# Two-layer decoder: the second batch's expert rows are gathered inside the first self unit, and VectorE alone normalizes the first batch

## The chip, the core and the metric

The kernel runs on one core of a Trainium2 chip. A core has a tensor engine for matrix products (PE, TensorE), a vector engine (DVE, VectorE), a scalar engine for activation functions (ACT, ScalarE), a general engine (POOL, GpSimd) and a sync engine (SP, SyncE) whose work here is to issue transfers. Each engine runs its own list of instructions in order and meets the others only through semaphores. Transfers (DMA) run beside them on 16 DMA engines. Products land in PSUM, eight banks of 128 x 512 floats here, and are copied ("evicted") to SBUF by ACT or DVE.

The metric is device time in microseconds (us). Before the change it is 2070.02 us, the median of three runs from 2069.47 to 2071.17. A difference of about 0.2% (4.1 us) is what a measurement of this kernel can tell from none.

## The reference, cut to what matters

All data are float32, with 4 batches of 512 tokens of width 256 and a second sequence ("context") of 1601 rows.

```python
x = layernorm(x + L0_attn(x))                       # a learning rule run over the tokens
x = layernorm(x + L0_xattn(x, ctx))                 # attention over the context
x = layernorm(x + L0_ffn(x))                        # 8 experts, the best 2 of each token
x = layernorm(x + L1_attn(x, w_qkv, w_out))         # causal self attention, 16 heads of 16
x = layernorm(x + L1_xattn(x, ctx, mask, ...))      # attention over the context, rotated, 16 heads
x = layernorm(x + L1_ffn(x))
```

The change sits at the seam between the third line and the fourth. The expert layer ends with a weighted sum of two rows per token,

```python
probs = softmax(xf @ Wr + br);  topw, topi = top_k(probs, 2);  topw = topw / sum(topw)
out[t] = topw[t, 0] * y[topi[t, 0], t] + topw[t, 1] * y[topi[t, 1], t]
```

and x + out is normalized (mean and variance over the 256 columns) before it becomes the input of the self attention,

```python
q, k, v = x @ w_qkv.T
attn = softmax(q @ k.T * 0.25 + causal_bias)        # per batch and head, 512 x 512
```

## The kernel before, in words

**Up to the seam.** The expert layer computes only the rows that were chosen and leaves them in memory (`ys`). The last layer is the function `last_layer` (line 1264). Its instructions are put out in an order written out by hand: what the Python code calls first stands first in each engine's list.

**Units.** The last layer is 32 units, each a batch and a group of 4 heads: first 16 self units (4 batches x 4 groups), then 16 cross units. This text counts them from 0, so units 0 to 3 are the first batch's self attention and unit 4 is the second batch's first. A self unit has 4 steps, one for each 128 keys. A step computes transposed scores of two heads at a time (`scores`, line 1572), adds the causal mask on the diagonal, takes the exponential on ACT (line 1582) and then the weighted sum of values on PE (`weighted`, line 1601).

The exponential needs the row maximum of the scores, so each unit's scores are also computed once ahead only for the maximum: 8 maximum steps per self unit (`slot1`, PE tile `most`, line 207; DVE lines 1531 and 1533), followed by `negated` (line 1546), which takes the maxima together and writes them by SP into the spare row of the query tile. The maximum steps run 4 steps ahead of the unit's end. So the first four maximum steps of unit n are issued in the second half of unit n-2 and the other four in the first half of unit n-1.

**Work between the steps.** Three lists belong to each unit. `starts` is done at its beginning (mostly loads by SP). `extras` is PE work spread evenly over its steps. `quiet` is work for other engines, one entry after each half step and the rest at the end. All of it stands in the same lists of the engines as the unit's own steps; nothing is moved later by a scheduler.

**What a batch needs before its self units.** `combined(b)` (line 1312) gathers the two expert rows of each token with indirect DMAs issued by POOL (line 1318), adds them with their weights on DVE (lines 1332 and 1345), normalizes (`normalize_apart`, line 152) and turns the result so that the width lies on the partitions: eight transposes on PE in two halves (line 1353), each half copied to SBUF by ACT (line 1356). In `normalize_apart` DVE counts the statistics, ACT takes the root by a logarithm and an exponential (`rstd_ln`, line 127) and ACT applies scale and shift (line 176). `rstd_newton` (line 135) is a root of twelve small DVE instructions used elsewhere in the kernel.

Then `self_rows(b, c)` (line 1371) computes keys and queries of half c of the heads (groups 2c and 2c+1), evicts them on ACT and writes them to memory by SP (`ksd`, `qd`, line 1293). A later load by SP (line 1296), the function `rows`, brings them back arranged by head into the tiles `ks` and `qt` of a group. The loads of half c overwrite the tiles of the batch before. `self_values(b)` (line 1388) makes the four value tiles.

**The start of the layer** (lines 1875 to 1901). POOL issues 8 gathers of the first batch and then 8 of the second. Meanwhile PE and ACT make the values and some keys of the context for the first batch: `context`, with `key` items evicted by ACT (line 1437) and then rotated on DVE or POOL (lines 1403 to 1406), and `value` items evicted by ACT (line 1451). Between them stands the load of ACT's function table (line 1886). Then comes one chain of the first batch in this order: two key items, the additions with statistics and the normalization, a key item, the turn, key and query products of half 0, a key item, the load of their rows. Behind it stand the context keys' rotations and writes, the batch's values, the additions of the second batch and the first eight value items of the next context. Then unit 0 begins with its first maximum steps.

**The later batches.** The second batch is normalized in the quiet list of unit 0, turned and multiplied (half 0) in the extras of unit 1, and its rows of half 0 are loaded at the start of unit 2. Its values and half 1 are in the extras of units 2 and 3, and the rows of half 1 are loaded at the start of unit 4. The third and fourth batches gather a quarter of the tokens at a time (`asked`, `summed`, two small buffers) in the quiet lists of two earlier units, with everything after that placed alike.

Of the kernel before, what the change touches and what calls it, by code (L numbers as in the profile page):

```python
# [17 lines left out]
P = 128  # L18
# [23 lines left out]
def decoder(ctx: ExitStack, tc: tile.TileContext, a: dict, out: bass.AP):  # L42
# [65 lines left out]
    def moments(r, n=NT):  # L108
        st = small.tile([P, NT, 6], F32, tag="st", name="st")
        mv = small.tile([P, NT, 2], F32, tag="mv", name="mv")[:, :n]  # L110
        for t in range(n):
            nc.vector.bn_stats(st[:, t, :], r[:, t, :])
        for t in range(n):
            nc.vector.bn_aggr(mv[:, t, :], st[:, t, :])
        return mv

# [1147 lines left out]
    def last_layer(causal):  # L1264

        with ExitStack() as s4:
# [45 lines left out]
            def combined(b):  # L1312

                ws = picks[b]

                def gather(y, t, k):
                    i = (2 * b + k) * NT + t
                    nc.gpsimd.indirect_dma_start(
                        y, None, ys, bass.IndirectOffsetOnAxis(ap=yrows[:, i : i + 1], axis=0)
                    )  # L1320

                def fetched(h):
                    y = p4.tile([P, 2, 512], F32, tag="ex", name="ex", bufs=4)
                    y = y.rearrange("p k (t d) -> p k t d", d=D)
                    for t in range(2):
                        for k in range(2):
                            gather(y[:, k, t, :], 2 * h + t, k)
                    state["y", b, h] = y

                def added(t):  # L1330
                    for k in range(2):
                        nc.vector.scalar_tensor_tensor(
                            out=x[b][:, t, :], in0=state["y", b, t // 2][:, k, t % 2, :],
                            scalar=ws[:, k, t : t + 1], in1=x[b][:, t, :], op0=ALU.mult, op1=ALU.add,
                        )

                def asked(t):
                    y = p4.tile([P, S], F32, tag="part", name="y").rearrange("p (k d) -> p k d", d=D)
                    for k in range(2):
                        gather(y[:, k, :], t, k)  # L1340
                    state["y", b, t] = y

                def summed(t):
                    for k in range(2):
                        nc.vector.scalar_tensor_tensor(
                            out=x[b][:, t, :], in0=state["y", b, t][:, k, :],
                            scalar=ws[:, k, t : t + 1], in1=x[b][:, t, :], op0=ALU.mult, op1=ALU.add,
                        )

                def turned(c):  # L1350
                    ps = one()
                    for t in range(NT):
                        nc.tensor.transpose(  # L1353
                            ps[:, t * P : (t + 1) * P], x[b][:, t, c * P : (c + 1) * P], ident
                        )
                    nc.scalar.copy(xT[b][:, c, :], ps)

                turns = [lambda c=c: turned(c) for c in range(2)]
                stats, pairs, ends = normalize_apart(x[b])
                if b > 1:  # L1360
                    ask = [lambda t=t: asked(t) for t in range(NT)]
                    add = [lambda t=t: summed(t) for t in range(NT)]
                    none = [lambda: None]
                    order = ask[:2] + none + add[:1] + ask[2:3] + add[1:2] + ask[3:] + none + add[2:3] + none + add[3:]
                    return order, pairs + ends, turns
                fetch = [lambda h=h: fetched(h) for h in range(2)]
                if b:
                    return fetch, [lambda t=t: added(t) for t in range(NT)], pairs + ends, turns
                return fetch, [lambda t=t: (added(t), stats(t)) for t in range(NT)] + ends, turns

            def self_rows(b, c, tile=raw_tile):

# [474 lines left out]

            for b in range(1, B):
                i = index[b - 1, 0, False]
                summed, *first_sums, normal, turn = combined(b)  # L1850
                if b == 1:
                    fetch1, (add1,) = summed, first_sums
                else:
                    quiet[i - 2] += summed[:8]
                    quiet[i - 1] += summed[8:]
                quiet[i] += normal
                for c in range(2):
                    items, rows = self_rows(b, c)
                    extras[i + 1 + 2 * c] += (turn if c == 0 else []) + items
                    starts[i + 2 + 2 * c].append(rows)  # L1860
                extras[i + 2] += self_values(b)
            for b in range(B):
                i = index[b - 1, 0, True] if b else index[B - 1, 0, False]
                for c in range(2):
# [14 lines left out]
            vals.append(values_tile(p4c, "v1", NKT, nc.vector))  # L1879
            for f in fetch:  # L1880
                f()
            for f in fetch1:
                f()
            for f in context(0, (), range(4), here=qt + kself):
                f()
            nc.scalar.preload_act_table_set(EXP_AND_LN)
# [9 lines left out]
            order = [apart(f) for f in keys0[0:2]] + add + [apart(keys0[4])] + turn + [k0_, q0_, apart(keys0[5]), rows0]  # L1896
            for f in order:
                f()
            for f in turns0 + self_values(0) + add1 + values1[:8]:
                f()  # L1900
            cosT, sinT = (p4c.tile([P, S2], F32, tag=n, name=n) for n in ("c_cos", "c_sin"))

# [263 lines left out]
```

## Time and profile before

| | |
|---|---|
| median of three runs | 2070.02 us (2069.47 to 2071.17) |
| the profiled execution's own time | 2090.35 us |
| its span | 2088.6 us |
| PE busy | 2020.8 us (97%) |
| DVE busy | 1144.2 us (55%) |
| ACT busy | 1082.4 us (52%) |
| POOL busy | 550.0 us (26%) |
| mean granted clock of PE | 0.983 |

In the span the last layer's start, from the first gather on POOL to the first maximum step on PE, runs from 893.52 to 937.64 us. Units 0 to 3 begin with their scores at 953.03, 972.94, 995.38 and 1016.36, unit 4 at 1037.5, so a self unit takes about 21 us. The start and these units are all that the change touches directly: some 145 us of the 2088.6.

A timeline's row gives start and duration in us, engine and line, operation, the tile written and the tiles read, shapes, how many equal instructions in a row it holds, and in brackets the idle time before and who ended it. A releaser "remote" is one that the trace could not put down to an instruction. SPq and ACTq are the DMA issues of these two engines. The page's row PEclk is the clock that the chip granted to PE, in tenths of full speed.

### The profile page before, as it was taken

The numbers are of one execution on the slowest core, as the hardware profiler recorded it, in microseconds if no ns is written. First come the engines' busy times: TensorE is split into PE (matmuls) and PEld (weight loads), VectorE is DVE, ScalarE is ACT, GpSimd is POOL, SyncE is SP. The second block draws the span as 40 slices with busy tenths as digits, with TensorE's granted clock in tenths as the row PEclk, the third lists the DMA queues.
The fourth block names the chain that finished last, engine by engine and source line by source line (L and its number), as shares of the span: only waits on it lengthen the run. The fifth ranks groups of instructions, "written<-read, shape, count | busy, mean of one in ns | idle before, by whom it ended". The sixth has DMA issues, their size and how long they took to land.

```text
span 2088.6 us, 34219 instructions
## 1 busy us (share of the span) xinstructions
PE 2020.8 (97%) x13090; PEld 1255.9 (60%) x13090; DVE 1144.2 (55%) x2845; ACT 1082.4 (52%) x2268; POOL 550.0 (26%) x504
## 2 busy tenths in 40 slices
PE   8999999998999999979999999999999999999998
PEld 5868677777998999954555554333333333333366
DVE  2434334451333233346666677777777878888234
ACT  1211222224564555534445535788778888888731
POOL 2010001121222222123410013465455344433100
PEclk9999999999999999999999989999999999999999
DMA  9910411116887786633421210112110111102000
GB/s 374 335 50 1 160 63 52 51 61 245 304 312 283 260 321 256 265 117 109 123 62 38 72 49 26 37 43 82 64 53 28 34 54 48 32 17 72 11 11 32
DMA packets 78990, 240.52 MB, mean 115 GB/s; under 512 B 14039, under 2 KB 36989, under 8 KB 66909
## 3 DMA queue, kind: packets, MB, share of 16 engines
q1 hardware_dynamic: 58828, 139.36, 19.5%
q0 software_dynamic: 13152, 85.64, 10.7%
q10 hardware_dynamic: 6832, 13.20, 1.9%
q8 instruction: 107, 1.75, 0.3%
q14 instruction: 71, 0.57, 0.1%
HBM read 192.37 MB, written 56.69 MB: 119 GB/s over the span
## 4 chain that ended last, share of the span: by engine, by line
PE 51%; DVE 2%; ACT 2%; DMA 1%; issue 1%; another core or an unknown queue 1%; SPq 0%; ACTq 0%; POOL 0%; DVEq 0%; POOLq 0%
PE s L1572 13%; PE one L207 12%; PE po L1601 12%; PE most L207 11%; PE one L1632 1%; PE s L1588 1%; ACT x L176 1%; DVE pm L1531 0%; PE one L1657 0%; DMA kcd<-raw 0%; DVE most L1533 0%; ACT ex L1582 0%; PE one L1353 0%; DVE st L161 0%
## 5 line engine op out<-in xcount | busy, mean ns | idle before, releaser
L1582 ACT ACTIVATE ex<-s 128x512 f32<-128x512 f32 (+4 forms) x1088 | 522.5, 565 | 231.2 <-PE s L1588 123.2
L1531 DVE TENSOR_REDUCE pm<-most 128x1 f32<-128x512 f32 x768 | 478.4, 683 | 104.6 <-PE most L207 103.2
L207 PE MATMUL most<-kc,qt 32*128 32x512 f32 (+1 forms) x2048 | 434.4, 538 | 1.3 <-ACT ot L1611 0.9
L1572 PE MATMUL s<-qt,kc 32*128 32x512 f32 (+1 forms) x1664 | 410.6, 618 | 0.0
L1618 POOL TENSOR_TENSOR ot<-ot,part 128x512 f32<-128x512 f32 x180 | 228.3, 1269 | 316.6 <-ACT part L1617 316.4
L1572 PEld LDWEIGHTS s<-qt,kc 32*128 32x128 f32 (+1 forms) x1664 | 134.3, 180 | 170.8 <-ACT ex L1582 122.2
L1601 PE MATMUL po<-ex,v 128*32 128x512 f32 (+1 forms) x1664 | 225.2, 605 | 0.4 <-ACT ex L1582 0.4
L207 PEld LDWEIGHTS most<-kc,qt 32*128 32x128 f32 x2048 | 174.6, 187 | 59.1 <-issue 20.8
L1062 DVE TENSOR_TENSOR g<-g,sg 128x1024 f32<-128x1024 f32 (+1 forms) x38 | 45.5, 1197 | 217.1 <-ACT sg L1060 217.1
L1533 DVE CUSTOM_DVE_ANT_0 most<-most,c_diagq 128x384 f32<-128x384 f32 (+3 forms) x256 | 118.6, 520 | 47.6 <-PE most L207 29.4
L207 PE MATMUL wide<-xbT,eWi 128*128 128x128 f32 (+1 forms) x928 | 136.7, 308 | 3.7 <-DVE xbT L1028 3.7
L207 PE MATMUL wide<-xbT,eWg 128*128 128x128 f32 (+1 forms) x928 | 133.7, 304 | 1.5 <-ACT g L1060 1.5
L207 PEld LDWEIGHTS wide<-xbT,eWi 128*128 128x128 f32 x928 | 127.0, 194 | 12.5 <-DVE xbT L1028 3.9
L207 PE MATMUL bank<-eWo,g 128*128 128x256 f32 x592 | 130.8, 379 | 0.0
L207 PEld LDWEIGHTS wide<-xbT,eWg 128*128 128x128 f32 x928 | 124.6, 191 | 8.3 <-ACT g L1060 1.7
L1601 PEld LDWEIGHTS po<-ex,v 128*32 128x32 f32 (+1 forms) x1664 | 34.5, 108 | 150.4 <-ACT ex L1582 144.9
L207 PEld LDWEIGHTS bank<-eWo,g 128*128 128x128 f32 x592 | 111.1, 190 | 14.4
L1617 ACT COPY part<-po 128x512 f32<-128x512 f32 x180 | 106.8, 594 | 7.1 <-PE po L1601 6.1
L1572 PE MATMUL s<-qt,ks 32*128 32x128 f32 (+3 forms) x512 | 106.4, 493 | 2.5 <-DVE pm L1533 0.8
L207 PE MATMUL most<-ks,qt 32*128 32x256 f32 (+3 forms) x512 | 89.9, 486 | 3.6 <-ACT v L1451 2.3
L1060 ACT ACTIVATE g<-wide,eWi 128x128 f32<-128x128 f32 (+1 forms) x232 | 70.6, 412 | 40.1 <-PE wide L207 39.5
L207 PE MATMUL wide<-ctxT,q 128*128 128x400 f32 (+1 forms) x256 | 88.7, 499 | 1.1 <-ACT xT L201 1.1
(331 smaller groups left out, 2843.8 us busy)
## 6 DMA issues: line engine op xcount, KB each, us to landing
xs<-zero SPq DMA_DIRECT2D x32, 512.0 KB
kc<-kcd SPq DMA_DIRECT2D x16, 800.5 KB
eWo<-in_eWo SPq DMA_DIRECT2D x8, 1408.0 KB
eWi<-in_eWi SPq DMA_DIRECT2D x8, 1028.0 KB
eWg<-in_eWg SPq DMA_DIRECT2D x8, 1028.0 KB
qt<-qd SPq DMA_DIRECT2D x32, 256.0 KB
ctxT<-in_ctxT SPq DMA_DIRECT2D x4, 1601.0 KB
kcd<-in_c_rowkc SPq DMA_DIRECT2D x4, 1601.0 KB
```

Of the source, the lines that this page charges most:

```text
L176: nc.scalar.activation(into(t), xb[:, t, :], AF.Identity, scale=mid["rs"][:, t : t + 1], bias=mid["nb"][:, t : t + 1],)
L207: nc.tensor.matmul(ps, l, r, start=(i == 0), stop=(i == n - 1))
L1060: nc.scalar.activation(dst[:, k, :], pv[:, k, :], func, bias=bias)
L1062: nc.vector.tensor_tensor(part, part, dst, ALU.mult)
L1531: nc.vector.tensor_reduce(pm[:, t, j, c : c + 1], ps, AX.X, ALU.max)
L1533: nc.vector.tensor_tensor_reduce(out=ps[:, :n], in0=ps[:, :n], in1=diagq[:, 384 - t * P : 384 - t * P + n], scale=1.0, scalar=LOWEST, op0= ...
L1572: nc.tensor.matmul(ps[:kn, q0:], kt[rows, k * P : k * P + kn], q2[rows, q0:], start=True, stop=cross)
L1582: nc.scalar.activation(ex[:kn, h, q0:], ps[:kn, q0:], AF.Exp)
L1588: nc.tensor.matmul(ps[:, k * P : (k + 1) * P], later_[:, :P], later_[:, P:], start=False, stop=True)
L1601: nc.tensor.matmul(po[j * 32 : j * 32 + 32, q0:], (vals if cross else vself)[b % 2][:kn, k, c0 : c0 + 32], ex[:kn, j % 2, q0:], start=True ...
L1617: nc.scalar.copy(part, po)
L1618: nc.gpsimd.tensor_tensor(state["ot"], state["ot"], part, ALU.add)
```

## The change

- The first batch: the statistics are counted with the additions as before, and one step `normal` does all the rest on DVE: moments, the root of twelve small instructions, and four applications of mean and scale. ACT's two root instructions, DVE's shift and ACT's four applications go. The two copies of its turned halves move from ACT to DVE.
- The second batch: its 8 gathers and 8 additions leave the start. They take the form of the later batches, a quarter of the tokens at a time through two small buffers, in the quiet list of unit 0. The statistics and normalization, unchanged on DVE and ACT, move from unit 0 to unit 1. The turn and the key and query products of half 0 move from unit 1 to unit 2, the load of their rows from the start of unit 2 to the start of unit 3, and the values from unit 2 to unit 3. Half 1 stays where it was.
- One consequence in the arithmetic: the first four maximum steps of unit 4 are still issued in unit 2, now ahead of the load of its rows, so these maxima come from the first batch's rows. A row's maximum is only subtracted before the exponential and cancels in the division, so the function computed stays the same.

Lines behind the new function are 6 higher after the change (the transposes stand on line 1359, the turned copies on 1362), and from `combined` on 19 higher.

```diff
+    def moments_of(st):
+        mv = small.tile([P, NT, 2], F32, tag="mv", name="mv")
+        for t in range(NT):
             nc.vector.bn_aggr(mv[:, t, :], st[:, t, :])
         return mv
...
-                    nc.scalar.copy(xT[b][:, c, :], ps)
+                    (nc.scalar.copy if b else nc.vector.tensor_copy)(xT[b][:, c, :], ps)
...
-                stats, pairs, ends = normalize_apart(x[b])
-                if b > 1:
+                _, pairs, ends = normalize_apart(x[b])
+                if b:
                     ask = [lambda t=t: asked(t) for t in range(NT)]
                     add = [lambda t=t: summed(t) for t in range(NT)]
                     none = [lambda: None]
                     order = ask[:2] + none + add[:1] + ask[2:3] + add[1:2] + ask[3:] + none + add[2:3] + none + add[3:]
                     return order, pairs + ends, turns
                 fetch = [lambda h=h: fetched(h) for h in range(2)]
-                if b:
-                    return fetch, [lambda t=t: added(t) for t in range(NT)], pairs + ends, turns
-                return fetch, [lambda t=t: (added(t), stats(t)) for t in range(NT)] + ends, turns
+                def normal():
+                    mv = moments_of(sums)
+                    rs = rstd_newton(mv)
+                    for t in range(NT):
+                        nc.vector.tensor_scalar(
+                            x[b][:, t, :], x[b][:, t, :], mv[:, t, 0:1], rs[:, t : t + 1], ALU.subtract, ALU.mult
+                        )
+                sums = small.tile([P, NT, 6], F32, tag="st", name="st")
+                def counted(t):
+                    added(t)
+                    nc.vector.bn_stats(sums[:, t, :], x[b][:, t, :])
+                return fetch, [lambda t=t: counted(t) for t in range(NT)] + [normal], turns
...
-                summed, *first_sums, normal, turn = combined(b)
-                if b == 1:
-                    fetch1, (add1,) = summed, first_sums
+                summed, normal, turn = combined(b)
+                first = b == 1
+                if first:
+                    quiet[i] += summed
                 else:
                     quiet[i - 2] += summed[:8]
                     quiet[i - 1] += summed[8:]
-                quiet[i] += normal
+                quiet[i + first] += normal
                 for c in range(2):
                     items, rows = self_rows(b, c)
-                    extras[i + 1 + 2 * c] += (turn if c == 0 else []) + items
-                    starts[i + 2 + 2 * c].append(rows)
-                extras[i + 2] += self_values(b)
+                    n = i + 2 * c + (first and c == 0)
+                    extras[n + 1] += (turn if c == 0 else []) + items
+                    starts[n + 2].append(rows)
+                extras[i + 2 + first] += self_values(b)
...
             for f in fetch:
                 f()
-            for f in fetch1:
-                f()
...
-            for f in turns0 + self_values(0) + add1 + values1[:8]:
+            for f in turns0 + self_values(0) + values1[:8]:
                 f()
```

More of the change, by code (lines that the diff above doesn't have):

```diff
@@ L113, in moments @@
         for t in range(n):
+            nc.vector.bn_aggr(mv[:, t, :], st[:, t, :])
+        return mv
+    def moments_of(st):
+        mv = small.tile([P, NT, 2], F32, tag="mv", name="mv")
+        for t in range(NT):
             nc.vector.bn_aggr(mv[:, t, :], st[:, t, :])
```

## The prediction

> **What bounds the kernel now.** I read the page's busy lines first, then the timelines of ACT, PE and DVE where the expert layer hands over to the last layer, then SP and PE around the first units. The page says that PE is the bound, so the change is worth what PE idles less or more.
>
> ```profile
> span 2088.6 us, 34219 instructions
> ...
> PE 2020.8 (97%) x13090; PEld 1255.9 (60%) x13090; DVE 1144.2 (55%) x2845; ACT 1082.4 (52%) x2268; POOL 550.0 (26%) x504
> ```
>
> The handover holds one of the longest idle times of PE. ACT's timeline there (start, duration, engine, line, operation, names, shapes, and in brackets the idle time before and who ended it):
>
> ```profile
> 902.74 0.38 ACT L1451 COPY v<-one 128x256 f32<-128x256 f32 x1 [1.66 <-PE one L207]
> 907.68 0.37 ACT L1451 COPY v<-one 65x256 f32<-65x256 f32 x1 [4.57 <-PE one L207]
> 908.07 1.28 ACT L1886 ACT_TABLE_LOAD   x1
> 914.04 0.69 ACT L1437 ACTIVATE raw<-one,bk 128x512 f32<-128x512 f32 x1 [4.69 <-remote]
> 916.11 0.69 ACT L1437 ACTIVATE raw<-one,bk 128x512 f32<-128x512 f32 x1 [1.38 <-remote]
> 916.70 0.29 ACT L130 ACTIVATE sd<-mv,eps 128x4 f32<-128x4 f32 x1
> ...
> 917.45 2.08 ACT L176 ACTIVATE x<-x,nb,rstd 128x256 f32<-128x256 f32 x4 [0.23 <-DVE nb L171]
> ```
>
> PE and DVE in the same stretch:
>
> ```profile
> 902.24 3.60 PE L207 MATMUL one<-qt,xaK 128*128 128x512 f32 x8
> 905.67 1.88 PE L207 MATMUL one<-ks,xaK 128*128 128x512 f32 x4
> 918.10 2.16 PE L1353 MATMUL one<-ident,x 128*128 128x128 f32 x5 [10.55 <-ACT x L176]
> ...
> 906.00 0.36 DVE L166 BATCH_NORM_AGGREGATE mv<-st 128x2 f32<-128x6 f32 x4
> ```
>
> DVE has the first batch's moments at 906.36, but the root and the scaling are on ACT, behind two key evictions (L1437). By the program the second of these waits for nothing but PE's semaphore, and its matmuls stand in the rows as ended at 905.83; the signal came at 916.09. PE's signals are late in this stretch from 902 on, and the rows show such lateness again at 998, 1020, 1065 and 1089 (0.7 to 1.8 us), each time next to indirect DMAs that POOL issues (16 in a row from 893.52 to 913.35 here). Whether this lateness exists when nothing is recorded decides the case.
>
> The second place is the load of a unit's rows. SP and PE at the change from unit 1 to unit 2, where the second batch's first rows are written and read back:
>
> ```profile
> 993.87 0.62 SPq L1293 DMA_DIRECT2D ksd<-raw  x1
> 995.59 0.61 SPq L1293 DMA_DIRECT2D qd<-raw  x1
> 998.15 0.34 SPq L1296 DMA_DIRECT2D ks<-ksd  x1
> 1000.91 0.33 SPq L1296 DMA_DIRECT2D qt<-qd  x1
> ```
>
> ```profile
> 993.00 1.88 PE L207 MATMUL one<-xT,qkvQ 128*128 128x512 f32 x4
> 994.81 0.64 PE L1601 MATMUL po<-ex,vs 128*32 128x256 f32 x8
> 995.38 0.70 PE L1572 MATMUL s<-qt,ks 32*128 32x512 f32 x2
> 995.39 0.49 PE L207 MATMUL most<-ks,qt 32*128 32x128 f32 x4
> ...
> 1006.80 0.59 PE L207 MATMUL most<-ks,qt 32*128 32x384 f32 x2
> ```
>
> From the end of the query product (994.88) over its eviction, the write, and the read back to the landing of qt (1003.55 by its semaphore's count) are 8.7 us. Nothing waits for it, because the first reader of these rows is the step at 1006.80 in the third quarter of unit 2.
>
> **The change part by part.**
>
> *Start of the layer.* After: twelve small DVE operations of the Newton root, one every 0.20 us in the rows near 1984 (busy 0.16 to 0.17 each), 2.4 us; four applications at 0.41 (the DVE TENSOR_SCALAR of 128x256, line 491), 1.6 us; so from 906.36 to 910.4. The last transpose of the first half ends at 910.6, DVE's copy of 128x512 from PSUM takes 0.69 (row of xbT, line 1028) to 911.3, the second to 912.0; the key product ends 0.86 later at 912.9. Then the dense PE work of the rows: query product and one key at 1.72, twelve value items at 0.863, 13.8 us, up to the first row maximum at 926.7. Before it is 937.71. The recorded gain is 11.0 us at full clock. Part of it is the half clock that before has from 912.96 to 923.2 (the stretch 918 to 924 has a granted clock of 0.57); PE after is idle from 907.55 to about 909.3 and could meet one half-clock window of 3.41 us as well, so the bounds are 7.6 and 11.0, and I take 10.
>
> Now the same start with PE's signals on time. ACT's second key eviction would begin at 905.9, and with the offsets of the rows (916.11 to 917.45 to 919.53) the applications run from 907.25 to 909.3; the queued key eviction (0.67) and the two copies (0.59 each) end at 911.2, the key product at 912.1. After it ends at 912.9. The change then *loses* 0.8 us here, bounds -0.5 and 2.
>
> Which of the two holds in the runs? The profiled execution's own time is 2090.35, the median is 2070.02: 20.3 us less when nothing is recorded. PE's matmuls are at full pace in the rows (0.429 us per 512 columns everywhere), so the 20 us must lie in stalls. The start's lateness with its half clock (about 10 us), 3 us at 471 to 473, and the smaller ones come to most of it. The rows of PE run on at an even pace while its signals wait, and backed-up signals then leave 35 to 40 ns apart; a slow PE would not look like this. I take it that most of the lateness belongs to the recording, at about two in three.
>
> [...]
>
> *Second batch's rows in unit 0.* Eight gathers leave the start; on POOL they are now queued behind the key rotations (947.39 to 956.94 in before's time), at 1.25 each. Issue to use is 4.1 us at the first gather (893.52 to 897.59), so the first pair is there by about 962.3, when DVE reaches the first addition (it idles until 963.58). The last pair is asked only after the second pair's additions and can hold DVE about 1.3 us at the end of the unit. Eight additions of 0.485 (up to 1.5 beside POOL) are 3.9 us on DVE, which is busy 10.85 of 20 us there; statistics, root and four applications on ACT move to unit 1. The additions that leave the start were hidden (DVE idle 4.03 us before 938.59). I take 0.5; bounds 0 and 4.
>
> *Turns and products one unit later.* Eight transposes and the key and query products (4.7 us of PE) go from unit 1 to 2, four value products (3.5) from 2 to 3. PE does them anyway. In unit 1 the products of the streamed context now come a quarter later and lose some of their 1.1 us wait (PE is idle from 979.5 to 980.63). I take -0.5; bounds -1.1 and 0.
>
> *The row load moves onto the path.* In the new order the second batch's key and query products stand in the last quarter of unit 2, and the load of ks and qt for heads' groups 0 and 1 at the start of unit 3. The remaining four of unit 4's eight maximum steps are issued during unit 3, the first right behind unit 3's first two score matmuls, and it waits for these two loads. Between the query product's end and that matmul PE has the weighted sum (0.57) and two scores (0.35 to 0.4), 1.0 us; the data come 7.9 (the second pair of groups in before: 1036.94 to 1044.84) to 8.7 us after the product. PE stands for 6.9 to 7.7 us, with everything behind this matmul in its queue: all of unit 3's scores, so ACT's exponentials and DVE's maxima too. SP's queue ahead of the loads holds unit 3's maxima rows and one kcd write, long released by then. After idle times of over 2 us before shows half-clock windows of 3.41 or 6.83 us (at 960.74 and at 912.96), 1.7 to 3.4 us of work lost. Unit 3 had about 1 us of small waits that the stall covers. I take 8.5; bounds 6 and 11.
>
> **Sum.** With the signals on time: 0.8 + 0.5 - 0.5 + 8.5 = 9.3, on the median 2070.0: 2079.3 us. In a profile, where the start's lateness goes: -10 + 0.5 - 0.5 + 8.5 = -1.5, own time near 2089. So I expect the profiled time to stay and the median to rise.
>
> **Rivals.**
> 1. *The late signals belong to the program.* For it: they come with the gathers, which are in every execution. Against: the 20 us and the even pace. Then the sum is -1.5 on the median, 2068.5, no measurable change (0.2%, 4.1 us, is about what this kernel's measurement can tell from none).
> 2. *Faster.* The same lateness is real, and it decides once unit 3's wait costs less than 5.9 us (10 less 4.1): with no half-clock window behind it and 1 us covered, 5.5, it is -4.5 or, with 11.0 at the start, -5.5: 2064.5 to 2065.5.
> 3. *Unit 3's wait is covered*, because the write and read back take less when DMA is idle or PE reaches that matmul later; with the start worth -0.8 the rest is 0.8: 2071. Against: three read-backs in before all took 7.9 to 8.7.
> 4. *DVE holds unit 0*: the additions at 1.0 to 1.5 us beside POOL, and the last pair late: 4 instead of 0.5, 2083.
>
> **How the numbers follow.** Forecast 0.54, rivals 0.13, 0.19, 0.07, 0.07. The second rival has more than the first because the read-backs' 7.9 to 8.7 us come from a recorded execution and may be shorter in an unrecorded one. The forecast's own range is 2075 to 2083 (bounds of the start and of unit 3). To hold 8 in 10 the range must take in rival 1 and the upper end of rival 2, so 2065 to 2083. Slower by over 0.2%: 0.52 of the forecast's 0.54 and rival 4, 0.59. Within: rivals 1 and 3 and the rest, 0.22. Faster: rival 2, 0.19.
>
> **What would show it.** In the profile after: line 1359's transposes start near 909.5 instead of 918.1; no run of 16 gathers, and ACT's key evictions without the two long waits; a wait of 7 us of PE at the first maximum step of unit 3, ended by the load of qt, and a lower granted clock behind it. Wrong if the profiled time and the median fall or rise alike (the lateness is then real), or if that matmul does not wait.

## The result, and the profile after

The change makes the kernel slower: 2085.07 us median (2080.43 to 2090.68, five runs) against 2071.05 us (2069.47 to 2071.34, five runs), a ratio of 1.0067 with a 95% interval of 1.0053 to 1.0081. The profiled execution's own time is 2090.68 us.

Every execution comes with its span and with the mean clock that PE was granted. Their product stands here as an estimate of the time that the execution would have taken at full clock, and the rest of the span as an estimate of what the clock cost. The text below uses the two as means over all executions of a kernel. Before has 2043.8 us and 24.8 us (33 executions on chip 6, below), after has 2052.4 us and 30.4 us (its five). So by this estimate about 8.6 us of the loss are work and waits, and 5.6 us are clock. The profiled execution of after is the slowest of its five.

The page of after, the same two lines as shown of before:

```profile
span 2088.9 us, 34224 instructions
...
PE 2021.8 (97%) x13090; PEld 1255.8 (60%) x13090; DVE 1150.1 (55%) x2862; ACT 1079.0 (52%) x2260; POOL 549.8 (26%) x504
```

The whole-span busy times tell nothing of it. The start of the layer does. PE and ACT of after:

```profile
902.18 4.48 PE L213 MATMUL one<-xaV,ks 128*128 128x256 f32 x20
...
909.93 1.88 PE L213 MATMUL one<-ks,xaK 128*128 128x512 f32 x4
911.96 1.65 PE L1359 MATMUL one<-ident,x 128*128 128x128 f32 x8 [0.15 <-DVE x L1378]
914.04 1.96 PE L213 MATMUL one<-xT,qkvK 128*128 128x512 f32 x4 [0.44 <-DVE xT L1362]
...
929.72 0.93 PE L213 MATMUL most<-ks,qt 32*128 32x384 f32 x8
```

```profile
906.69 0.37 ACT L1470 COPY v<-one 65x256 f32<-65x256 f32 x1 [0.49 <-PE one L213]
907.08 1.28 ACT L1905 ACT_TABLE_LOAD   x1
908.46 0.69 ACT L1456 ACTIVATE raw<-one,bk 128x512 f32<-128x512 f32 x1
910.13 0.69 ACT L1456 ACTIVATE raw<-one,bk 128x512 f32<-128x512 f32 x1 [0.98 <-PE one L213]
```

The value products end at 906.66 and ACT evicts the last at 906.69: no signal of PE is late here. The wait of 10.55 us ahead of the transposes is 0.15 us. Then the units. PE of after in units 2 and 3, and SP with the row loads:

```profile
994.59 0.37 PE L1591 MATMUL s<-qt,ks 32*128 32x256 f32 x1
997.50 1.21 PE L1591 MATMUL s<-qt,ks 32*128 32x256 f32 x2 [2.53 <-DVE at L1655]
...
1006.83 1.88 PE L213 MATMUL one<-xT,qkvQ 128*128 128x512 f32 x4
1008.64 0.64 PE L1620 MATMUL po<-ex,vs 128*32 128x256 f32 x8
1009.21 1.13 PE L1591 MATMUL s<-qt,ks 32*128 32x512 f32 x4
1016.82 0.83 PE L213 MATMUL most<-ks,qt 32*128 32x128 f32 x8 [6.49 <-DMA qt<-qd]
```

```profile
1007.70 0.61 SPq L1299 DMA_DIRECT2D ksd<-raw  x1
1009.42 0.58 SPq L1299 DMA_DIRECT2D qd<-raw  x1
1012.38 0.34 SPq L1302 DMA_DIRECT2D ks<-ksd  x1
1014.06 0.33 SPq L1302 DMA_DIRECT2D qt<-qd  x1
```

From the query product's end (1008.71) to the maximum step that waits for qt (1016.82) are 8.1 us, and PE stands for 6.49 of them, a little less than the 6.9 to 7.7 forecast. The wait of 2.53 us in unit 2 was not forecast. The granted clock is below 1 in both units. The windows of after over units 0 to 3, one line each: start and end, length, busy time of PE, weight loads, DVE, ACT and POOL with their instructions, the granted clock (1.00 is full, and half clock is 0.50), DMA share and GB/s:

```profile
945.10:963.10 18.00, 16.64 (x116) 10.15 (x117) 11.86 (x44) 7.25 (x20) 11.31 (x16) 0.81 0.72 239
963.10:981.70 18.60, 17.04 (x132) 8.65 (x132) 13.51 (x56) 10.12 (x27) 3.44 (x3) 1.00 0.23 65
981.70:1009.20 27.50, 24.38 (x148) 12.57 (x144) 17.69 (x51) 10.58 (x25) 23.62 (x21) 0.88 0.31 86
1009.20:1041.30 32.10, 24.55 (x158) 13.71 (x154) 14.20 (x49) 10.49 (x27) 5.78 (x9) 0.84 0.43 123
```

The profile of before that stands with the prediction could not serve for comparison, as the experiments show. The same table of a later profiled execution of before (label e12_before_third), whose time of 2070.35 us is near the median:

```profile
940.40:958.70 18.30, 15.71 (x116) 9.13 (x116) 10.79 (x48) 9.53 (x26) 3.72 (x8) 0.91 0.55 185
958.70:981.20 22.50, 21.18 (x151) 10.98 (x148) 12.56 (x47) 10.14 (x25) 10.20 (x9) 1.00 0.21 57
981.20:1002.50 21.30, 20.29 (x148) 11.50 (x144) 15.83 (x49) 9.93 (x25) 15.78 (x15) 1.00 0.62 190
1002.50:1020.90 18.40, 17.42 (x140) 9.52 (x136) 13.44 (x49) 8.34 (x22) 6.68 (x10) 1.00 0.27 75
```

Line by line, after less before: units 0 and 1 together are 4.2 us shorter, because work left unit 1; unit 2 is 6.2 us longer and unit 3 13.7 us. The four units take 96.2 us instead of 80.5. PE's busy time in them is 82.6 against 74.6, for nearly as many matmuls (554 and 555); by the granted clocks of the rows, 0.81, 0.88 and 0.84 against one 0.91, this is by estimate mostly the half clock. The idle rest, 13.6 against 5.9, is the waits. The start, from PE's first value product to its first maximum step, is 36.21 us (893.51 to 929.72) against 36.89 (888.16 to 925.05). These two executions are 20.3 us apart, more than the medians; 5.35 us of that lie ahead of the first value product, where the two kernels do the same.

### The profile page after: what moved, and what is told of

Its sections match the earlier page's. It is cut to its first block, busy times and chain, and to the rows that moved or that the text cites. A ratio compares the mean times of both kernels' runs of the same rounds, so it can differ in the third digit from the quotient of the medians.

```text
span 2088.9 us, 34224 instructions
## 1 busy us (share of the span) xinstructions
PE 2021.8 (97%) x13090; PEld 1255.8 (60%) x13090; DVE 1150.1 (55%) x2862; ACT 1079.0 (52%) x2260; POOL 549.8 (26%) x504
## 5 line engine op out<-in xcount | busy, mean ns | idle before, releaser
L690 POOL DMA_INDIRECT xs<-x,rows x32 | 31.0, 968 | 222.8 <-DVE rs L842 175.7
```

The source lines that it names most:

```text
L690: nc.gpsimd.indirect_dma_start(xs, bass.IndirectOffsetOnAxis(ap=rows[:, k * NT + t : k * NT + t + 1], axis=0), x[b][:, t, :], None)
```

## The experiments

Times are medians; "full clock" and "clock loss" are the means explained above, for the kernel and, in brackets, for the runs of before beside it.

| label | chip | time, us (runs) | before beside it (runs) | ratio, 95% interval | full clock | clock loss |
|---|---|---|---|---|---|---|
| e1_before_again | 6 | 2067.89 (12) | 2070.64 (33) | 0.9987, 0.9975 to 0.9999 | 2043.9 (2043.8) | 22.7 (24.8) |
| e2_products_first | 6 | 2078.77 (10) | same | 1.0039, 1.0026 to 1.0052 | 2049.0 | 27.6 |
| e3_dve_normalizes | 6 | 2068.21 (12) | same | 0.9988, 0.9974 to 1.0001 | 2042.8 | 23.9 |
| e4_rows_not_later | 6 | 2077.19 (12) | same | 1.0032, 1.0017 to 1.0048 | 2044.5 | 30.6 |
| e5_maxima_later | 10 | 2081.22 (12) | 2070.85 (35) | 1.0046, 1.0029 to 1.0063 | 2047.4 (2043.1) | 31.9 (26.0) |
| e6_postponed_only | 10 | 2080.35 (12) | same | 1.0050, 1.0032 to 1.0068 | 2052.3 | 27.7 |
| e7_normal_in_unit1 | 10 | 2070.57 (12) | same | 0.9997, 0.9981 to 1.0014 | 2044.5 | 24.3 |
| e8_first_and_later | 10 | 2078.26 (12) | same | 1.0038, 1.0021 to 1.0056 | 2048.8 | 28.6 |
| e9_after_again | 4 | 2090.17 (12) | 2089.05 (29) | 1.0017, 0.9999 to 1.0034 | 2057.3 (2053.5) | 32.6 (33.6) |
| e10_third_later | 4 | 2085.92 (12) | same | 0.9987, 0.9975 to 1.0000 | 2053.6 | 30.9 |
| e11_all_three | 4 | 2082.01 (12) | same | 0.9970, 0.9953 to 0.9986 | 2051.6 | 29.1 |
| e12_before_third | 9 | 2069.62 (10) | 2069.47 (25) | 0.9994, 0.9983 to 1.0006 | 2042.6 (2043.4) | 25.0 (24.8) |
| e13_dve_normalizes | 9 | 2068.42 (10) | same | 0.9989, 0.9975 to 1.0004 | 2043.1 | 23.4 |
| e14_normal_in_unit1 | 9 | 2070.64 (10) | same | 1.0005, 0.9991 to 1.0019 | 2044.3 | 25.0 |
| e15_dve_normalizes | 9 | 2069.08 (10) | 2070.76 (18) | 0.9998, 0.9986 to 1.0010 | 2043.7 (2044.0) | 24.0 (24.5) |
| e16_normal_in_unit1 | 9 | 2071.08 (10) | same | 1.0008, 0.9994 to 1.0023 | 2044.4 | 26.1 |

The first row compares a kernel with itself and gives 2.75 us between medians, with an interval that leaves out 1. So much may happen by chance here.

**Before, once more.** No edit.

> The kernel before, once more, for a second profile of it. Theory A (the late signals of PE and the long start belonged to that one profiled execution): the new profile's own time lies near the median, 2070 to 2075, no signal is late by more than 0.3 us beside the gathers, the transposes of line 1353 start near 909 instead of 918, unit 0 near 944 and unit 3 near 1005. Theory B (the lateness belongs to the program): the same long start again, unit 0 near 953, unit 3 near 1016, the profile's own time near 2090 only if the rest of it is disturbed too.

Its profiled execution took 2074.09 us, the slowest of its own twelve, and no signal of PE is late. The transposes begin at 908.45, unit 0 at 943.32 and unit 3 at 1007.11. So theory A holds as far as the long start is concerned: the first profile of before showed something that the twelve executions on this chip, with 2064.67 to 2074.09 us, leave no room for.

**The products ahead of the context keys.**

```diff
-                extras[i + 2] = keys1[n : n + 3] + extras[i + 2]
+                extras[i + 2] = extras[i + 2] + keys1[n : n + 3] if i == 0 else keys1[n : n + 3] + extras[i + 2]
```

> After, with one thing different: in unit 2 the turn and the key and query products of the second batch stand ahead of the three context key items instead of behind them. Theory A (unit 3's wait for the row load is what the change costs): the products end some 6 us earlier, the loads of ks and qt then wait only for the last maximum step of unit 2 that reads the old rows, PE's wait at the first maximum step of unit 3 falls from 6.5 us to 0 to 2, the half-clock window behind it (10.2 us, 5 us of work) goes too, and the time falls by 6 to 11 us to 2074 to 2079. Theory B (the loss lies in the additions in units 0 and 2 and in DVE's queue): the time stays within 3 us of after, 2082 to 2088.

The time is within theory A's 2074 to 2079, but not by the way that was expected. The wait of unit 2 is gone, and that of unit 3 is still 4.75 us. SP's queue in this kernel shows why:

```profile
990.40 0.61 SPq L1299 DMA_DIRECT2D qd<-raw  x1
991.11 6.46 SPq L1299 DMA_DIRECT2D kcd<-raw  x3
997.68 0.39 SPq L1302 DMA_DIRECT2D ks<-ksd  x1
998.16 0.38 SPq L1302 DMA_DIRECT2D qt<-qd  x1
```

The loads stand in SP's queue behind three writes of context keys, the last of which is issued at 997.6. Earlier products gained little, partly because a write for other work came between them and their load. From the load of qt to the step that waits for it are then 6.1 us (998.16 to 1004.28), against 2.8 in after; no run separates why. By the ratios to before, 1.0067 became 1.0039.

**VectorE's normalization alone.** The first half of the change on before: one step `normal` on DVE and DVE's copies; gathers, additions and the second batch as before.

```diff
+                return fetch, [lambda t=t: counted(t) for t in range(NT)] + [normal], turns
-                return fetch, [lambda t=t: (added(t), stats(t)) for t in range(NT)] + ends, turns
```

> Before, with the first half of the change alone: VectorE normalizes the first batch and copies its turned tiles; the second batch stays as it was. Theory A (signals are on time in ordinary runs): a loss of 0.8 us, bounds -0.5 and 2, so 2070 to 2073, the same within what can be told. Theory B (signals are late beside the gathers): the start gains 7 to 11 us, 2060 to 2064.

No measurable change, 0.9988. Chip 9 gave the same twice (e13_dve_normalizes and e15_dve_normalizes in the table).

**Gathers in unit 0, nothing postponed.**

```diff
-                quiet[i + first] += normal
+                quiet[i] += normal
-                    n = i + 2 * c + (first and c == 0)
+                    n = i + 2 * c
-                extras[i + 2 + first] += self_values(b)
+                extras[i + 2] += self_values(b)
```

> After, with the second batch gathered and added inside unit 0 but normalized there too, turned and multiplied in unit 1 and loaded at the start of unit 2 as in before. Theory A: unit 3 has no wait; what is left is the start (0.8) and DVE's longer end of unit 0 (0.5 to 4), 2071 to 2075. Theory B (the moved gathers and additions are the loss): at least half of the 14 us stay, 2077 or more.

Neither theory fits: the time is that of theory B, but less than half of the 14 us stay. At full clock it is near before (2044.5 against 2043.8), so the moved gathers and additions cost hardly any work; the clock loss is 5.8 us higher. Its profile shows one wait that before lacks, early in unit 1, where PE waits for a maximum on DVE behind the normalization:

```profile
957.74 0.70 PE L1591 MATMUL s<-qt,ks 32*128 32x512 f32 x2 [0.93 <-DVE pm L1552]
...
962.78 3.14 PE L213 MATMUL one<-xaV,cx 128*128 128x256 f32 x8 [3.05 <-DVE pm L1552]
```

One half-clock window of 3.41 us follows in that execution, which was one of the quickest (2072.52). Where the slower executions lost their clock isn't in a trace.

**The waiting maximum steps moved.**

```diff
-                            reduces.append([next1()])
+                            reduces.append([] if i == 3 and k == 0 else [next1()])
+                        if i == 3 and k == 1:
+                            reduces[half].append(next1())
```

> After, with the wait of unit 3 taken away by its work: the two maximum steps of unit 4 that stand in the first step of unit 3 are issued in its second step, two a half step, some 8 us later, when the rows have landed. Theory A (the wait at that maximum step costs 6.5 us of standing PE, and the throttle takes another part behind it): PE's wait of 6.5 us is gone, span times clock falls from 2052 to 2045 to 2047, the share lost to the clock from 30 us to 25 to 28, the time to 2071 to 2077. Theory B (the wait only collects time that is lost anyway, to the context keys or to DVE behind it): span times clock stays above 2050 and the time above 2080.

The wait moved with the steps and kept 4.96 us. At full clock the kernel is 4.3 us above before beside it, where after was 8.6 above, so about half came back; of the clock loss nothing did. SP's rows show that the load had become slower:

```profile
1001.49 0.58 SPq L1299 DMA_DIRECT2D qd<-raw  x1
1004.06 0.34 SPq L1302 DMA_DIRECT2D ks<-ksd  x1
1008.41 0.33 SPq L1302 DMA_DIRECT2D qt<-qd  x1
```

The load of qt is issued 6.9 us after the write of qd, against 4.6 us in after. POOL's gathers for the third batch were issued at 998.52 to 1002.32 here, right beside the write; in after they came at 1003.89 to 1007.68. That the gathers slowed the write is likely but was not isolated.

**The postponement alone.** On before, with all 16 gathers at the start and ACT's normalization:

```diff
-                quiet[i] += normal
+                first = b == 1
+                quiet[i + first] += normal
-                    extras[i + 1 + 2 * c] += (turn if c == 0 else []) + items
-                    starts[i + 2 + 2 * c].append(rows)
+                    n = i + 2 * c + (first and c == 0)
+                    extras[n + 1] += (turn if c == 0 else []) + items
+                    starts[n + 2].append(rows)
-                extras[i + 2] += self_values(b)
+                extras[i + 2 + first] += self_values(b)
```

> Before, with the second half of the change's postponement alone: gathers and additions of both batches stay at the start, ACT normalizes both, but the second batch is normalized in unit 1, turned and multiplied in unit 2, its rows loaded at the start of unit 3 and its values made there. Theory A (the postponed load is the cause): unit 3 waits 5 to 7 us at its first maximum step as after does, span times clock rises by 5 to 8 us over before's 2044, the time to 2076 to 2083. Theory B (the moved gathers and additions are a cause of their own): less than half of after's loss, 2073 or less.

This is the decisive run. The postponement alone has both waits of after, with no gather moved:

```profile
996.74 1.22 PE L1572 MATMUL s<-qt,ks 32*128 32x256 f32 x2 [2.55 <-DVE at L1636]
...
1008.55 1.13 PE L1572 MATMUL s<-qt,ks 32*128 32x512 f32 x4
1016.43 0.83 PE L207 MATMUL most<-ks,qt 32*128 32x128 f32 x8 [6.75 <-DMA qt<-qd]
```

It costs 9.2 us at full clock, as much as the whole change (8.6), and its interval for the ratio overlaps that of the change. Its clock loss rises by 1.7 us only, against 5.6 for after; that difference isn't explained.

**All but the postponement.** As the variant of e4, but with the normalization left in unit 1.

```diff
-                    n = i + 2 * c + (first and c == 0)
+                    n = i + 2 * c
-                extras[i + 2 + first] += self_values(b)
+                extras[i + 2] += self_values(b)
```

> After with the second batch gathered and added in unit 0, normalized in unit 1 as in after, but turned and multiplied in unit 1 and loaded at the start of unit 2 as in before. It takes away the wait of 3.05 us at the start of unit 1 that the variant with everything normalized at the end of unit 0 had. Theory A (idle times of 2 to 3 us bring the throttle, and that variant lost 6 us more to the clock than before for its one wait): the share lost to the clock falls from 30.6 to 24 to 27, span times clock stays at 2043 to 2046, the time is 2067 to 2072. Theory B (the gathers beside the units bring the lower clock, wait or not): the loss to the clock stays near 30, the time 2074 to 2078.

2070.57 us, a ratio of 0.9997: the whole loss is gone. Unit 2 takes 20.6 us and unit 3 18.4. The clock loss is 24.3 us: with e4's wait of 3.05 us its clock loss is gone too, as theory A had it, though what links the two is not in a trace. On chip 9 (e14_normal_in_unit1) the same kernel gave 1.0005.

**Both edits on after**, products first and maximum steps later.

> After with both edits: the second batch's turn and products ahead of the context keys in unit 2, and the two maximum steps of unit 4 moved to the second step of unit 3. Theory A: neither the wait of unit 2 behind DVE's queue (2.5 us) nor that of unit 3 is there, span times clock 2042 to 2045, the time 2066 to 2071, no slower than before. Theory B: as without them, above 2076.

Missed. The wait for the load is 0.65 us, but behind it PE stands 2.35 us for an addition on DVE (line 1633) and 1.20 us for a maximum:

```profile
1003.96 0.50 PE L213 MATMUL most<-ks,qt 32*128 32x128 f32 x8 [0.65 <-DMA qt<-qd]
1007.41 0.84 PE L1591 MATMUL s<-qt,ks 32*128 32x384 f32 x1 [2.35 <-DVE ot L1633]
1011.49 3.43 PE L213 MATMUL one<-xT,qkvK 128*128 128x512 f32 x4 [1.20 <-DVE pm L1552]
```

Moving the steps put twice as many maxima into one step; that this made DVE late there is likely, not shown. Full clock 2048.8, no better than with the products first alone.

**A chip with late signals.** The next three were meant to price the waits one by one; the first is after without an edit.

> The kernel after, once more, on the chip of the next two. Theory A (two waits of PE, 2.5 us in unit 2 behind DVE's additions for the third batch and 6.5 us in unit 3 behind the row load, and the half clock behind them): span times clock 2051 to 2054, the loss to the clock 28 to 31 us, the time 2080 to 2086, both waits in the profile. Theory B (the first measurement of after was a bad draw): 2075 or less.

> After, with the third batch's first three quarters gathered and added in unit 3 instead of unit 2. Theory A (in unit 2 DVE is held by these additions, which wait for their gathers and run beside POOL's rotations; in the same unit the gathers lengthen the row load): the wait of 2.5 us in unit 2 goes, the one in unit 3 shrinks to 4 to 6, span times clock falls by 3 to 5 us to 2047 to 2050, the time to 2074 to 2080. Theory B (that wait comes from the context keys or from PE being earlier): it stays at 2 to 3 us and the time at 2080 or above.

> After with three edits: products of the second batch ahead of the context keys in unit 2, the two maximum steps moved to the second step of unit 3, the third batch's additions in unit 3. Theory A (these waits are all that the postponement costs): no wait of PE over 1.5 us in units 2 and 3, span times clock 2043 to 2046, the time 2067 to 2073, as before. Theory B (something else in the postponed order costs too): 2075 or more without such a wait.

The edit of e10 is one line; e11 has it together with the two edits of e8:

```diff
-                    quiet[i - 2] += summed[:8]
+                    quiet[i - 2 + (b == 2)] += summed[:8]
```

They fell on a chip where before takes 2089.05 us (29 executions, 2082.93 to 2097.39), near the 2090.35 of its first profile. After takes 2090.17 us there: no measurable change. The times of the expectations don't fit such a chip, and the waits only in part. After itself (e9, the first two rows) waits 1.10 us in unit 2 here, not 2.5, and 8.51 us in unit 3. In e10 no wait of over 0.3 us is left in unit 2, while that of unit 3 (the third row) is 7.66 us and not 4 to 6; full clock falls by 3.7 us, as theory A had it.

```profile
998.31 0.69 PE L1591 MATMUL s<-qt,ks 32*128 32x256 f32 x2 [1.10 <-DVE at L1655]
1017.10 0.83 PE L213 MATMUL most<-ks,qt 32*128 32x128 f32 x8 [8.51 <-DMA qt<-qd]
1009.56 0.83 PE L213 MATMUL most<-ks,qt 32*128 32x128 f32 x8 [7.66 <-DMA qt<-qd]
```

In e11 the wait for the load is 0.24 us; PE waits 1.02 and 1.49 us for DVE in these units, and the kernel is 0.9970 of before.

ACT of e9_after_again shows the late signals. PE's value products end in its rows at 904.17 (start 899.69, 4.48 us):

```profile
902.48 0.38 ACT L1470 COPY v<-one 128x256 f32<-128x256 f32 x1 [0.49 <-issue]
904.52 0.37 ACT L1470 COPY v<-one 128x256 f32<-128x256 f32 x1 [1.67 <-PE one L213]
906.66 0.37 ACT L1470 COPY v<-one 65x256 f32<-65x256 f32 x1 [1.76 <-PE one L213]
```

The last eviction begins 2.5 us behind the product that it waits for; in after on the first chip this was 0.03 us. Before the change begins, an eviction starts at 475.20, 4.2 us behind its product (ended at 471.04), beside nine gathers in a row. In the first profile of before, with 16 gathers in a row, the second key eviction begins 10.3 us behind its product (905.83 to 916.11). So the start gains 10.6 us between these two profiles (46.70 to 36.11 us from the first value product to the first maximum step), and units 0 to 3 give it back: 97.3 us in e9 (944.23 to 1041.56) against 84.5.

**Which half shortens the start there?** Five runs asked this of another chip: before unchanged (e12), the kernel of e3 (e13 and e15) and that of e7 (e14 and e16).

> The kernel before. On a chip where it takes near 2089: PE's signals are late by 5 us or more around the 16 gathers and the first maximum step comes 44 us after the first gather. On a chip where it takes near 2070: no signal late by over 0.3 us and about 35 us.

> Before with VectorE's normalization and copies alone, all 16 gathers at the start. Where signals are late: the copies of the turned tiles wait for PE's late signals as ACT's evictions did, and less than half of the 10 us come back, 2084 to 2090. Where they are on time: as before within 3 us.

> After without the postponed products and loads: eight gathers at the start, eight in unit 0, the second batch normalized in unit 1. Where signals are late: the start is 8 to 11 us shorter than before's and nothing is lost in unit 3, 2077 to 2082 against 2089. Where they are on time: as before within 3 us.

> Before with VectorE's normalization and copies alone, all 16 gathers at the start. Where before takes near 2089 (late signals): the copies wait for PE's late signals as ACT's evictions did, and less than half of the 10 us come back, 2084 to 2090. Where it takes near 2070: as before within 3 us.

> After without the postponed products and loads. Where before takes near 2089 (late signals): a start 8 to 11 us shorter and nothing lost in unit 3, 2077 to 2082. Where it takes near 2070: as before within 3 us.

Both times this fell on chip 9, where signals are on time. VectorE's normalization alone and all of the change but the postponement are both free where signals are on time; what shortens the start on a chip with late signals stays open. No version here is measurably faster than before on the chips with signals on time. Against after's 1.0067, e7's order is 12 to 14 us faster by its three ratios to before (0.9997, 1.0005 and 1.0008).

## Why the prediction was wrong

The direction was right and the size was not: 2079.3 was forecast, 2085.07 came, 2.1 us above the range. The forecast sum was +9.3 us and the median moved by 14.0. It took the start with signals on time, and the runs of after have them; but the reason given, the recording, was wrong, so that part was luck. By stage, from the two tables above:

- **Start of the layer.** Forecast 0.8 lost, with -0.5 to 2 as bounds. Measured 36.21 against 36.89 us, 0.7 gained. In the later profile of before the first transposes wait 0.37, 0.16, 0.16 and 0.16 us for ACT's applications, which I had not counted.
- **Second batch's rows in unit 0.** Forecast 0.5; unit 0 is 0.3 us shorter. The additions took 0.48 us each there, as forecast.
- **Turns and products one unit later.** This is the step that failed. It said "PE does them anyway" and costed -0.5, with bounds of -1.1 and 0. With 4.7 us moved out of unit 1 and 3.5 us moved from unit 2 to 3, unit 1 should be 17.8 and is 18.6; unit 2 should be 22.5 and is 27.5. That is 5.8 us. Of the 5.0 us in unit 2, 2.53 are the wait for DVE, and the half clock that runs on behind it, from 997.50 to 1003.79, takes about 3.1 more, an estimate: half of its 6.29 us.
- **The row load moves onto the path.** Forecast 8.5, with 6 and 11 as bounds. Unit 3 should be 21.9 us (18.4 and the 3.5 of the values) and is 32.1: 10.2 us: 6.49 are the wait, and the half clock behind it, from 1016.82 to 1024.26, takes about 3.7, half of its 7.44 us by the same estimate. The mechanism, the place and the instruction were right, the size within the bounds.

-0.7 - 0.3 + 5.8 + 10.2 is 15.0 us for these two executions; with the 5.35 us ahead of the start it is their whole difference. That it lies near the 14.0 us between the medians is partly chance, since after's execution lost more to the clock than its others.

What happened in unit 2? DVE of after in unit 2:

```profile
991.95 3.90 DVE L1351 SCALAR_TENSOR_TENSOR x<-y,ws,x 128x256 f32<-128x256 f32 x2 [1.12 <-DMA y<-ys,yrows]
995.77 0.17 DVE L1568 TENSOR_REDUCE nm<-pm 128x16 f32<-128x16 f32 x1
995.97 0.21 DVE L1576 STREAM_TRANSPOSE nrows<-nm 128x32 f32<-128x32 f32 x1
996.12 0.01 DVE L1422 LOAD_MASK_SELECT swp<-raw  x1
996.12 0.72 DVE L1422 STREAM_SHUFFLE swp<-raw 128x512 f32<-128x512 f32 x1
996.74 0.24 DVE L1654 RECIPROCAL rd<-one 128x16 f32<-128x16 f32 x1
997.02 0.42 DVE L1655 TENSOR_TENSOR at<-one,rd 128x256 f32<-128x256 f32 x1
```

The same additions in the later profile of before:

```profile
989.78 2.33 DVE L1345 SCALAR_TENSOR_TENSOR x<-y,ws,x 128x256 f32<-128x256 f32 x2
```

The third batch's first additions belong to unit 2 in both kernels. PE reaches unit 2 earlier against POOL once work has left unit 1: POOL's first gather for them is issued 5.2 us into unit 2 (986.89 against 981.74), where in before it stood 3.3 us ahead of it (977.91 against 981.21). Unit 1 is 3.9 us shorter, and its context key products also come later in it, as the prediction said: 11.5 and 16.1 us into the unit (974.57, 979.26) instead of 7.7 and 10.0 (966.47, 968.70). POOL rotates these keys ahead of the gathers. The prediction booked this only as a gain. So DVE waits 1.12 us for the rows, and the two additions take 3.90 us beside POOL's rotations, against 2.33 us in the later profile of before. The division that ends unit 1 (line 1655) is queued behind them on DVE, and PE's next scores wait for it. I had checked who waits for the products that moved, but not who was kept in time by their being in unit 1. That the third batch's additions hold DVE fits e10, where they are moved and the wait is gone; but on that chip it was only 1.10 us, and the 2.53 us on the first chip were not tried without them. They are not the cause alone: in e2 they stay in unit 2, PE has the moved products to do meanwhile, and that wait is gone too.

The same additions take less when POOL is idle: four take 1.92 us together at the end of unit 0's list in after (at 963.48), and two take 3.90 us here, beside POOL's rotations. What makes them longer there was not shown.

**The clock** was in the forecast with 1.7 to 3.4 us, for one window of 3.41 or 6.83 us behind unit 3's wait. The two windows that the prediction names for this, at 960.74 and 912.96 of before, are 6.83 and 10.24 us long. In after's profile half-clock windows stand at 996.96 (6.83 us) and at 1014.02 (10.24 us), and over all executions the clock loss is 30.4 us against 24.8. The waits of 6.49 us and more in unit 3 (6.49 in after, 6.75 in e6, 7.66 in e10, 8.51 in e9) all came with half clock: the eight maximum products behind them took 0.83 us, against 0.50 in e8 behind a wait of 0.65 us. Shorter waits came with and without it. In after it began 2.0 us into the wait of 2.53 us in unit 2. A wait of 2.90 us ahead of the first value product came without it in the first profile of before, where the 32 products behind it took 7.14 us, but with 3.41 us of it in e12_before_third, where they took 8.83. A window of 6.83 us at 1689.86 of after follows an idle time of only 0.44 us. So among these waits, from 0.44 to 2.90 us, the length alone does not decide it; what does stays open.

**Late signals: recording or program?** I gave two to one for the recording, from the 20.3 us between the profile's own time and the median. This was wrong, and so was the alternative as I put it. All executions carry their span and clock, and the profiled ones are not slower as a class (in e2 and e10 the profiled one was the quickest, in e1 and after the slowest). The lateness goes with the chip: one of the four showed it, in all three profiles there (an eviction of context values comes 2.5 us late in e9, 2.5 in e10 and 1.9 in e11), and before took 2082.93 to 2097.39 us in all of 29 executions. All these were taken within one series of runs on that chip, so whether it lasts isn't shown. The first profile of before and the times beside it can't have been taken under the same conditions; that it came from such a chip is the likeliest reading, not a shown one. That recording holds PE's signals back is shown by no run. Nor is PE's pace in that first profile 0.429 us per 512 columns everywhere, as the prediction has it: the four key products at 920.73, at half clock, took 3.19 us together, against 1.98 in e12_before_third. The second sum, -1.5 us where signals are late, was close: +1.1 us on chip 4, 1.0017 of before. It was close by errors that cancel, since between the two profiles the start gained 10.6 us, near the forecast, and the units lost some 13 instead of 8.5. That the profiled time would stay and the median rise came true (2090.35 and 2090.68) by luck: the first is of an execution with late signals, the second is the slowest of five executions on a chip without them.

Of the rivals, the first (late signals that are real, no measurable change) is what chip 4 shows. The second, faster, came nowhere. The third, that unit 3's wait is covered, is refuted by the 6.49 us. The fourth, DVE holding unit 0, did not come in after, but e4 shows such a wait, 3.05 us early in unit 1.

## What to carry to other kernels

When work is moved to a later stage of an in-order schedule, two things have to be read: the round trip of the moved data to its first reader (here 8.1 us through memory to a step that was due 1.6 us later), and what other engines did during the stage that became shorter, because their work then comes late against it (here unit 1 was 3.9 us shorter, and POOL's first gather came 5.2 us into unit 2 instead of 3.3 us ahead of it). A profile whose own time lies 1% from the median of the runs (here 2090.35 against 2070.02 us) may show something that these runs do not have, as here a wait of 10.55 us; before anything is built on a wait in it, that execution should be repeated. A wait on the engine that bounds the kernel cost more than its length here: about 3.1 us of half clock by estimate behind the 2.53 us in unit 2, about 3.7 behind the 6.49 us in unit 3. With the mean clock at hand, the product of span and clock gives an estimate of the wait apart from what the clock adds.

## What was unexpected of the hardware

- On one of four chips the signals of PE came late beside POOL's indirect DMAs, up to 4.2 us in e9_after_again, and before took 2089 us instead of 2070. On two of the other three the last eviction of context values begins 0.03 us (after, chip 6) and 0.04 us (e12, chip 9) behind its product; on the third, chip 10, before took 2070.85 us.
- Executions of one kernel on one chip spread by 5 to 20 us (2066.03 to 2070.91 for e13, 2066.31 to 2086.75 for before on chip 10). With 10 to 12 executions of a kernel the intervals above reach 0.12 to 0.18% to either side, 2.5 to 3.7 us.
- The clock loss can differ between kernels of equal full-clock time (2044.5 us both): 30.6 us in e4 on chip 6, 24.3 in e7 on chip 10, which differ in where one normalization is issued.
